# Filling the edge tile of x1 on VectorE behind the third block's candidates, instead of on GpSimd and VectorE ahead of step 1

## The chip, the cores and the metric

The kernel runs on one core of a Trainium2 chip. The core has five engines, each with its own instruction stream that it works through in order: TensorE (PE in the profile, with PEld for its weight loads), VectorE (DVE), ScalarE (ACT), GpSimd (POOL) and SyncE (SP). An instruction that needs another engine's result waits for that engine's semaphore, and everything behind it in its own stream waits with it. The metric is the device time of one execution in microseconds (us), smaller being better.

## The reference

A graph network with two layers works on 2708 nodes with 256 features. Cut to what matters here:

```python
# layer 0
x = _layernorm(x + relu(concatenate([x, adj @ x], axis=1) @ weight + bias))
# layer 1: two steps
R = S + eye(N);  R = R / R.sum(-1, keepdims=True)      # S is adj again
for n in range(2):
    q = Xa @ W1.T @ W2.T;  k = Xa @ W3.T
    probs = softmax(q @ k.T)
    # keep, in each row, the largest probabilities until their sum reaches 0.9
    A = probs * mask;  A = A / A.sum(-1)
    Xf = R @ Xf;  Xa = A @ Xa
    Z = Z + Xf @ U1[n].T + Xa @ U2[n].T
h = X + Z                                              # then two layer norms
```

The output of layer 0 is called x1 below. The product `A @ Xa` of the first step, with `Xa = x1`, is where the tile of this change is used.

## The kernel before, in words

**Tiling.** The 2708 nodes are cut into NB = 22 blocks of 128 rows. The last block, number EDGE = 21, has only 20 rows. `x1` is one tile of 128 partitions by 22 blocks by 256 features. A weight block `e` holds one row block of attention weights, 128 by 2708, padded to 2720 columns. For a product on TensorE it must be transposed in pieces of 128 columns. `columns(e, k)` cuts them out; the last piece starts at 2720 - 128 = 2592, so that the 20 last nodes lie in it at places 96 to 115 (AT = 96). The matching right-hand side can't be `x1[:, 21, :]`, in which these rows lie at partitions 0 to 19. So there is a second tile, `x1_edge`, 128 by 256, which is zero but for the 20 last rows of x1 at partitions 96 to 115. `part_y` (L566) takes it as the right-hand side of the last piece; the profile calls it `yg`, since it is cut out of the same room as the tile `yg`.

**The room.** `y_room` (L504) lies where layer 0's input `xT` lay. It holds the two buffers of `yg` for the sparse product, some spare columns, and `x1_edge`. The names of the second `Lists` use the second buffer of `yg` as well.

**Stages.** Layer 0 runs first, over the 22 blocks in a loop that ends at L499. While it runs, the columns of the adjacency matrix that hold anything are named, and two objects `Lists` (blocks 0 to 15, blocks 16 to 21) collect these names. `lists.end()` of the first one, right behind the loop, writes the names through memory: VectorE computes the target places `to` (L350), GpSimd sends seven scatters (L354), each of which waits until the one before it has landed, and then loads the finished list into `ix` (L357). Next come the lines of this change (L508, L509). Then step 1 begins, and after it step 2.

**The order around the change** is written out by hand: a manual schedule keeps, on each engine, the order in which the program names its instructions. The framework only adds the waits that the data need. The head of step 1 (L896 to L909) is this, where `begin1(t, 2)` writes three pairs of logits (TensorE L527, copied out by ScalarE L534) with six calls of `u1_project` in between (TensorE L670, ScalarE L673, and two stores by SyncE L674, L675):

```python
    begin1(0, 2)
    extract1(0)
    begin1(1, 2)
    part = exps1(0)
    part(0), part(1)
    begin1(2, 2)
    lists.take(0, 2)
    ra = finish1(0)
    extract1(1)
    part = exps1(1)
    part(0), part(1)
    for t in range(n_u, NB):
        u1_project(t)
    extract1(2)
```

`extract1(t)` is VectorE's: the eight largest of each of 16 segments of a row (L589, the "candidates"), their maximum (L613, L615) and 64 of them in order (L596, L598). `exps1(t)` is ScalarE's: the exponentials of these (L630) and of the whole row (L632), which need that maximum. `lists.take` is VectorE's (L330, L331), for the second list. `finish1(t)` is VectorE's: sums over the ordered values (L646 to L653), and the cut of the row at its threshold (L654). Its L651 reads column 0 of `sums`, the tile `xs`, which GpSimd clears once at L603, behind everything of `lists.end()`.

Behind this head the loop over the 22 blocks begins: in each pass TensorE transposes one block of weights (L554), ScalarE copies the pieces out (L556), and TensorE multiplies them by x1 (L583), while logits, exponentials and thresholds of the next blocks go on. GpSimd gathers the named rows of the adjacency matrix for the sparse product (L376, two blocks for each of the first two passes, one for each pass behind them), adds the identity (L378), and SyncE loads and stores its tiles (L373 to L390).

Of the kernel before, what the change touches and what calls it, by code (L numbers as in the profile page):

```python
# [41 lines left out]
AT = 96  # L42
# [19 lines left out]
def gnn_two_layer_kernel(ctx: ExitStack, tc: tile.TileContext, N, xT_d, x_d, adj_d, w0_d, b0_d,  # L62
# [72 lines left out]
    with fast:  # L135
        fast_path(fast, tc, c, flags, fint, xT_d, x_d, w0_d, b0_d, w1_d, w2_d, w3_d, u1_d, u2_d, g_d, b_d)
# [22 lines left out]
def fast_path(ctx, tc, c, flags, fint, xT_d, x_d, w0_d, b0_d, w1_d, w2_d, w3_d, u1_d, u2_d, g_d, b_d):  # L159
    nc = tc.nc  # L160
    N, D, DA, NB, DC, KH, CHS, rows = c.N, c.D, c.DA, c.NB, c.DC, c.KH, c.CHS, c.rows
# [66 lines left out]
    x1 = big.tile([P, NB, D], FP, tag="x1", name="x1")  # L228
# [11 lines left out]
    EDGE = NB - 1  # L240
# [264 lines left out]
    yg = y_room[:, :YW].rearrange("p (s c d) -> p s c d", s=2, d=D)  # L505
    spares = [y_room[:, YW + D * i:YW + D * (i + 1)] for i in range(4)]
    x1_edge = y_room[:, YW + 4 * D:YW + 5 * D]
    nc.gpsimd.memset(x1_edge, 0.0)  # L508
    nc.vector.tensor_copy(x1_edge[AT:AT + rows(EDGE)], x1[:rows(EDGE), EDGE, :])  # L509
    lists = Lists(ML, NB, flags[:, NF - 2:], yg[:, 1].rearrange("p c d -> p (c d)"))  # L510
    lists.turn()
    x1_transpose(NB - 1)
# [73 lines left out]
    def seg_max(dst, src, p, step, width):  # L586
        for i in range(NS):
            w = min(width, N - SEG * i) if step == SEG else width
            nc.vector.max(dst[:p, i * 8:(i + 1) * 8], src[:p, i * step:i * step + w])  # L589

    def put_in_order(dst, n, cand, p):

        spare = small.tile([P, NS2 * 8], FP, tag="spare", name="spare", bufs=1)[:, :cand.shape[1]]
        src = cand
        for i in range(0, n, 8):
            nc.vector.max(dst[:p, i:i + 8], src[:p])  # L596
            if i + 8 < n:
                nc.vector.match_replace(spare[:p], dst[:p, i:i + 8], src[:p], -3.0e38)  # L598
                src = spare
# [6 lines left out]
    def extract1(t):  # L606
        p = rows(t)
        e = es[t % 4]
        cand = small.tile([P, NS2 * 8], FP, tag="cand", name="cand", bufs=2)[:, :NS * 8]
        seg_max(cand, e, p, SEG, SEG)  # L610
        cv = cand.rearrange("p (s k) -> p s k", k=8)
        nmax = small.tile([P, 1], FP, tag="nmax", name="nmax", bufs=3)
        nc.vector.tensor_reduce(nmax[:p], cv[:p, :, 0], AX.X, ALU.max, negate=True)  # L613
        srt = small.tile([P, TOP1 + 1], FP, tag="srt", name="srt", bufs=3)
        nc.vector.tensor_reduce(srt[:p, TOP1:], cv[:p, :, 7], AX.X, ALU.max)  # L615
        put_in_order(srt, TOP1, cand, p)
        st1[t] = (nmax, srt)
# [48 lines left out]
    def u1_project(t):  # L666
        p = rows(t)
        pz = ps_acc()
        for j in range(DC):
            nc.tensor.matmul(pz[:p], lhsT=x1T[:, j, t * P:t * P + p],  # L670
                             rhs=c.u1[:, j].rearrange("p s e -> p (s e)"), start=j == 0, stop=j == DC - 1)
        o = v_out[:p, t % VS]
        nc.scalar.copy(o.rearrange("p s d -> p (s d)"), pz[:p])  # L673
        nc.sync.dma_start(out=c.yf_d[:p, t, :], in_=o[:, 1, :])  # L674
        nc.sync.dma_start(out=c.v_d[:p, t, :], in_=o[:, 0, :])  # L675
# [231 lines left out]
    for t in range(n_u, NB):  # L907
        u1_project(t)
    extract1(2)  # L909
    ends = None  # L910

    at = {(m // 2, 3 * (m % 2) + 1): m for m in range(4)}
# [844 lines left out]
```

## Time and profile before

| what | value |
|---|---|
| median of 3 runs | 1281.5 us (1278.85 to 1284.95) |
| the profiled execution's own time | 1286.8 us |
| its span (first to last instruction) | 1284.9 us |
| mean granted TensorE clock | 0.975 of full speed |
| PE busy | 1202.1 us, 94% |
| DVE busy | 973.9 us, 76% |
| ACT busy | 735.1 us, 57% |
| POOL busy | 634.9 us, 49% |

Step 1's head lies between about 280 and 348 us of the span, and the 22 passes follow. In the stretch from 312 to 325 us PE is busy for 0.36 us. Rows of the timeline give the start, the duration, the engine, the line and operation, the output and the input tile, how many instructions are merged, and in brackets how long the engine sat idle before it and who released it. Rows of the waits give who waited for whom: us in total, how often, and the longest. L12 is line 12 of the kernel file.

### The profile page before, as it was taken

The page shows a single profiled execution, that of the slowest core. Times are in us where ns is not written, and L with a number is a line of the kernel's source. Part 1 is how long each engine was busy: PE and PEld are TensorE (multiplying, and loading weights), DVE is VectorE, ACT ScalarE, POOL GpSimd, SP SyncE. Part 2 cuts the span into 40 slices and gives each one's busy share as a digit, 9 for nine tenths or more (in the row PEclk, how much of TensorE's full clock was granted, in tenths as well). Part 3 has the DMA queues.
Part 4 walks back from the last instruction along what each step waited for, and adds up shares of the span by engine and source line. Part 5 has one row for each costly group of instructions (what it writes and reads, how often), then busy time and mean ns, then how long its engine had stood idle before and what let it go on. Part 6 is the DMA issues. An engine that isn't in the chain of part 4 may idle for free.

```text
span 1284.9 us, 18709 instructions
## 1 busy us (share of the span) xinstructions
PE 1202.1 (94%) x5772; PEld 904.3 (70%) x5772; DVE 973.9 (76%) x3253; ACT 735.1 (57%) x1299; POOL 634.9 (49%) x597
## 2 busy tenths in 40 slices
PE   8999999987799999999999978999998999999885
PEld 6888888842377777777777646777766777776664
DVE  2455554973999998988871278979878999999886
ACT  2000111032566666666665498887888999989821
POOL 1000000004076552577766068878774878888860
PEclk9999999989899999999999888999999999999997
DMA  7455544523322220133334154665664555555451
GB/s 197 149 197 172 160 151 153 172 82 98 100 80 92 61 68 32 41 94 94 91 89 107 50 152 152 181 187 178 183 150 122 173 160 163 169 185 160 144 135 39
DMA packets 101703, 165.99 MB, mean 129 GB/s; under 512 B 17362, under 2 KB 74070, under 8 KB 101594
## 3 DMA queue, kind: packets, MB, share of 16 engines
q1 hardware_dynamic: 75308, 108.65, 26.1%
q0 software_dynamic: 20544, 51.17, 14.8%
q10 hardware_dynamic: 5742, 4.89, 1.3%
q8 instruction: 48, 0.79, 0.3%
q14 instruction: 61, 0.50, 0.1%
HBM read 130.74 MB, written 33.90 MB: 128 GB/s over the span
## 4 chain that ended last, share of the span: by engine, by line
PE 71%; DVE 10%; ACT 7%; DMA 6%; issue 3%; POOL 2%; SPq 0%; POOLq 0%; ACTq 0%; DVEq 0%
PE acc L583 23%; PE acc L266 16%; PE lg L527 8%; PE misc L769 6%; PE tr L554 6%; DMA yg<-yf_d,ix 3%; PE acc L670 2%; DMA yg<-v_d,ix 2%; DVE e L1110 2%; PE misc L402 2%; ACT e L988 2%; PE acc L691 2%; PE misc L441 2%; PE misc L719 2%; PE acc L477 1%
## 5 line engine op out<-in xcount | busy, mean ns | idle before, releaser
L556 ACT COPY wT<-tr 128x512 f32<-128x512 f32 (+2 forms) x258 | 136.6, 537 | 205.8 <-PE tr L554 205.8
L583 PE MATMUL acc<-ya,wT 128*128 128x256 f32 x924 | 223.1, 383 | 0.0
L739 POOL DMA_INDIRECT yg<-v_d,ix x154 | 193.5, 1256 | 59.3 <-issue 25.3
L583 PE MATMUL acc<-x,wT 128*128 128x256 f32 x882 | 217.4, 386 | 0.0
L739 POOL DMA_INDIRECT yg<-yf_d,ix x154 | 190.7, 1239 | 48.3 <-issue 26.2
L266 PE MATMUL acc<-y,adj_t 128*128 128x257 f32 x924 | 206.1, 382 | 0.0
L769 PE MATMUL misc<-yg,adj_t 128*128 128x256 f32 (+1 forms) x704 | 187.9, 398 | 18.1 <-DMA yg<-yf_d,ix 7.2
L583 PEld LDWEIGHTS acc<-x,wT 128*128 128x128 f32 x882 | 159.0, 190 | 58.1 <-issue 24.7
L583 PEld LDWEIGHTS acc<-ya,wT 128*128 128x128 f32 x924 | 172.1, 191 | 38.2 <-issue 16.7
L266 PEld LDWEIGHTS acc<-y,adj_t 128*128 128x128 f32 x924 | 174.9, 191 | 27.3 <-issue 1.9
L376 POOL DMA_INDIRECT adj_t<-in_adj,ix x154 | 168.4, 1094 | 50.9 <-issue 39.5
L769 PEld LDWEIGHTS misc<-yg,adj_t 128*128 128x128 f32 (+1 forms) x704 | 123.6, 191 | 69.6 <-issue 23.2
L527 PE MATMUL lg<-k,q 64*128 64x512 f32 (+3 forms) x528 | 138.0, 600 | 27.4 <-ACT e L534 13.5
L554 PE MATMUL tr<-ident,e 128*128 128x128 f32 (+1 forms) x946 | 145.2, 272 | 6.9 <-ACT wT L556 4.6
L554 PEld LDWEIGHTS tr<-ident,e 128*128 128x128 f32 (+1 forms) x946 | 117.7, 141 | 40.5 <-ACT wT L556 8.8
L343 POOL DMA_DIRECT2D part_d<-e x1 | 0.6, 573 | 278.6 <-DVE e L342 278.6
L988 ACT ACTIVATE e<-e,st 128x2708 f32<-128x2708 f32 (+1 forms) x43 | 113.5, 2640 | 0.1
L991 ACT ACTIVATE e<-e,st 128x2708 f32<-128x2708 f32 (+1 forms) x42 | 111.0, 2642 | 0.1
L454 ACT COPY x1T<-tr 128x256 f32<-128x256 f32 (+1 forms) x22 | 8.0, 365 | 179.8 <-PE tr L453 179.8
L589 DVE MAX8 cand<-e 128x8 f32<-128x170 f32 (+1 forms) x352 | 86.9, 318 | 15.9 <-ACT e L534 15.7
L1052 DVE MAX8 cand<-w 128x8 f32<-128x170 f32 (+1 forms) x352 | 94.1, 321 | 0.0
L527 PEld LDWEIGHTS lg<-k,q 64*128 64x128 f32 (+1 forms) x528 | 39.3, 183 | 59.1 <-issue 20.7
(246 smaller groups left out, 1749.6 us busy)
## 6 DMA issues: line engine op xcount, KB each, us to landing
adj_t<-in_adj SPq DMA_DIRECT2D x44, 704.0 KB
adj_t<-adjc_d SPq DMA_DIRECT2D x44, 448.0 KB
adjc_d<-adj_t SPq DMA_DIRECT2D x22, 256.0 KB
base<-za_d SPq DMA_DIRECT2D x40, 128.0 KB
adjc_d<-adj_t SPq DMA_DIRECT2D x22, 192.0 KB
xt<-in_x ACTq DMA_DIRECT2D x21, 128.0 KB
x_d<-x SPq DMA_DIRECT2D x21, 128.0 KB
x1b_d<-xb SPq DMA_DIRECT2D x21, 128.0 KB
```

The lines of the kernel that those rows point to most:

```text
L266: nc.tensor.matmul(acc[:p, :n], lhsT=halves[k // KH][:, k % KH, :p], rhs=y[:, k, :n], start=k == 0, stop=stop and k == NB - 1)
L376: nc.gpsimd.indirect_dma_start(out=a[:CW, i, :], out_offset=None, in_=adj_rows, in_offset=bass.IndirectOffsetOnAxis(ap=ix[:CW, m, i:i + 1] ...
L527: nc.tensor.matmul(lg[:p, h, at:at + b - a], lhsT=q[o, t * P:t * P + p], rhs=keys[s][o, i, :b - a], start=True, stop=True)
L554: nc.tensor.transpose(tr[:, k % 4, :p], columns(e[:p], k), ident[:p, :p])
L556: nc.scalar.copy(wT[:, :len(ks), :p], tr[:, :len(ks), :p])
L583: nc.tensor.matmul(acc[:p, :D], lhsT=wT[:, k % 4, :p], rhs=part_y(y, k), start=k == 0, stop=k == NB - 1)
L589: nc.vector.max(dst[:p, i * 8:(i + 1) * 8], src[:p, i * step:i * step + w])
L739: nc.gpsimd.indirect_dma_start(out=y[:CW, i, :], out_offset=None, in_=rows_d, in_offset=bass.IndirectOffsetOnAxis(ap=ix[:CW, m, i:i + 1], ...
L769: nc.tensor.matmul(acc[:p, :D], lhsT=a[:kw, k, :p], rhs=y[:kw, k, :], start=k == 0, stop=k == CC)
L988: nc.scalar.activation(scr[:b.p, :N], e, AF.Relu, bias=b.nz, scale=b.l[k], accum_out=b.relu)
L991: nc.scalar.activation(scr[:b.p, :N], e, AF.Sign, bias=b.nz, scale=b.l[k], accum_out=b.sign)
L1052: nc.vector.max(b.cand[:p, 8 * i:8 * i + 8], low[:p, SEG2 * i:SEG2 * (i + 1)])
```

## The change

The two instructions that fill `x1_edge` move. Before, GpSimd clears the tile (L508) and VectorE copies the 20 rows (L509), right behind the first `lists.end()` and ahead of step 1. After, VectorE does both, behind `extract1(2)`, the third block's candidates, just ahead of the loop over the blocks (L908 and L909 of the changed file; lines between the two places lie two lines higher there).

```diff
@@ -505,8 +505,6 @@
     yg = y_room[:, :YW].rearrange("p (s c d) -> p s c d", s=2, d=D)
     spares = [y_room[:, YW + D * i:YW + D * (i + 1)] for i in range(4)]
     x1_edge = y_room[:, YW + 4 * D:YW + 5 * D]
-    nc.gpsimd.memset(x1_edge, 0.0)
-    nc.vector.tensor_copy(x1_edge[AT:AT + rows(EDGE)], x1[:rows(EDGE), EDGE, :])
     lists = Lists(ML, NB, flags[:, NF - 2:], yg[:, 1].rearrange("p c d -> p (c d)"))
     lists.turn()
     x1_transpose(NB - 1)
@@ -907,6 +905,8 @@
     for t in range(n_u, NB):
         u1_project(t)
     extract1(2)
+    nc.vector.memset(x1_edge, 0.0)
+    nc.vector.tensor_copy(x1_edge[AT:AT + rows(EDGE)], x1[:rows(EDGE), EDGE, :])
     ends = None
 
     at = {(m // 2, 3 * (m % 2) + 1): m for m in range(4)}
```

## The prediction

> **What bounds the kernel now.** I read the page first. The fourth part, the chain that ended last, says that TensorE sets most of the time:
>
> ```profile
> PE 71%; DVE 10%; ACT 7%; DMA 6%; issue 3%; POOL 2%; SPq 0%; POOLq 0%; ACTq 0%; DVEq 0%
> ```
>
> So a change is worth what it does to stretches in which PE stands still, and the edit touches one. The waits between 285 and 400 us:
>
> ```profile
> DVE yg L509 <- POOL xs L603: 19.6, 1, 19.6
> ...
> PE lg L527 <- ACT e L534: 13.5, 2, 13.0
> ```
>
> These two are ends of one stall handed from engine to engine. The timelines of GpSimd, VectorE, ScalarE and TensorE show it:
>
> ```profile
> 292.02 0.93 POOL L354 DMA_INDIRECT list_d<-e,to  x1 [2.96 <-DVE to L350]
> ...
> 307.38 0.84 POOL L354 DMA_INDIRECT list_d<-e,to  x1 [1.39 <-DMA list_d<-e,to]
> 309.63 1.24 POOL L357 DMA_DIRECT2D ix<-list_d  x1 [1.41 <-DMA list_d<-e,to]
> 310.86 0.32 POOL L508 MEMSET yg<- 128x256 f32 x1
> 311.11 0.11 POOL L603 MEMSET xs<- 128x1 f32 x1
> ```
> ```profile
> 291.42 0.21 DVE L350 SCALAR_TENSOR_TENSOR to<-run,before_m,e 16x7 int32<-16x7 f32 x1
> 311.22 0.56 DVE L509 COPY yg<-x 20x256 f32<-20x256 f32 x1 [19.58 <-POOL xs L603]
> 311.79 3.88 DVE L589 MAX8 cand<-e 128x8 f32<-128x170 f32 x16
> ...
> 325.50 0.28 DVE L651 SCALAR_TENSOR_TENSOR qs<-xs,sc,srt 128x64 f32<-128x64 f32 x1
> ```
> ```profile
> 307.75 0.59 ACT L673 COPY v_out<-acc 128x512 f32<-128x512 f32 x1 [1.17 <-PE acc L670]
> 321.22 0.35 ACT L630 ACTIVATE srt<-srt,nmax 128x65 f32<-128x65 f32 x1 [12.88 <-DVE srt L596]
> ```
> ```profile
> 308.66 3.70 PE L670 MATMUL acc<-u,x1T 128*128 128x512 f32 x8
> 325.33 2.08 PE L527 MATMUL lg<-k,q 64*128 64x512 f32 x4 [12.96 <-ACT e L534]
> 327.34 4.56 PE L670 MATMUL acc<-u,x1T 128*128 128x512 f32 x8
> ...
> 342.11 5.46 PE L670 MATMUL acc<-u,x1T 128*128 128x512 f32 x8 [2.40 <-ACT v_out L673]
> ```
>
> GpSimd clears the tile at 310.86 only because the clear stands behind seven scatters that wait for one another. VectorE's copy waits for the clear, and behind the copy stands all of `extract1(0)`. ScalarE has nothing left but `exps1(0)`, which needs `extract1(0)`. TensorE has run until 312.36 and can't write the next logits, because ScalarE, stuck in front of `exps1(0)`, has not copied the last ones out. The chain of waits in order of time agrees: it runs through the clear, L509, L589, the sorting, L632, L654, the next L589 and the exponentials until 342.11, and from there on is nearly all PE.
>
> **The change part by part.** *The wait that goes.* VectorE is free at 291.63 (291.42 + 0.21). `extract1(0)` also needs its logits; ScalarE's last copy of them ran from 290.32 for 0.71, to 291.03. So it starts at about 291.6 instead of 311.79, and takes the same 9.3 us (311.79 to 321.10): done at 301.0. `lists.take` follows (321.10 to 323.5 before, 2.4 us) and ends at 303.4. So VectorE gains 20 us, but not all of it counts.
>
> *Who is late next.* ScalarE's order holds the six copies of `begin1(1, 2)` ahead of `exps1(0)`; the last of them ends at 308.34 (307.75 + 0.59), paced by TensorE. `exps1(0)` can't start before, and no longer has to wait: 308.34 instead of 321.22. **The gain is 321.22 - 308.34 = 12.9 us**; of VectorE's 20 us the other 7 become an idle wait for ScalarE. From there each row moves up by 12.9: the exponentials end at 311.5, `finish1(0)` starts at 311.5 (its first row stands at 324.41, 0.90 us idle behind ScalarE's L632), `extract1(1)` ends at 325.4 (338.31 before), `exps1(1)` starts at 325.5 (338.43), and the last two projections of TensorE, which wait for the copies behind `exps1(1)`, at 342.11 - 12.9 = 329.2.
>
> *TensorE in this stretch.* It loses the 13 us hole: the next logits start at 312.5, right behind 312.36. They and the following six projections then run warm: 1.13 for 2.08 and 3.70 for 4.56 us, 1.8 us less. That gives nothing, since 329.2 is set by ScalarE: the hole of 2.40 us before the last projections only grows, to 2.4 + 1.8 = 4.2 us or a little less. Sum of the holes, 15.4 before and about 4.2 after, and 1.8 of cold clock: 11.2 + 1.8 = 13.0, the same gain counted from the other side.
>
> *The clock behind the longer hole.* The row at 342.11 shows eight matmuls in 5.46 us where 3.70 is usual, so already the 2.40 us hole costs 1.76; the granted clock is 0.79 from 340 to 348 us. [...] I take 0. [...]
>
> *The two instructions in their new place.* The clear on VectorE: no row clears SBUF there, but L182 clears 128x257 in PSUM in 0.27 us; GpSimd's own clear took 0.32. The copy stays at 0.56. Together 0.83 us behind `extract1(2)`, whose end is 347.61 - 12.9 = 334.7; so `finish1(1)`, queued behind it, begins at 335.5 and ends at 340.2. What waits for it is the transposing of block 1, at 362.61 - 12.9 = 349.7, so 9.5 us of cover. `extract1(3)` waited 0.18 us for its logits, so 0.65 us of delay goes on; passes take PE 17.0 us, of which VectorE is busy 16.2, so it is gone after a pass or so. `x1_edge` itself is read first by L583 acc<-yg at 364.74 - 12.9 = 351.9, 16 us after the copy. Price: 0; without the cover 0.8.
>
> *GpSimd's side.* The removed clear frees 0.25 us. A wait remains that the clear used to hide: L651 of `finish1(0)` needs the cleared `xs`, which stands behind the same scatters. It is cleared at about 310.9 to 311.0. L651 falls 1.09 us behind the start of `finish1(0)`: 312.6. **So 1.6 us of cover**, and from there on each us by which the scatters get later costs one. Before, they ran beside an idle VectorE; now `extract1(0)` and `lists.take` run beside them. The nearest row for that is the first gather of the adjacency rows (313.91 to 322.4), which ran beside the same L589, L596, L598 and L330: all seven took 0.94 to 1.01 us, 0.30 apart. So I take no stretch. The other end is the second list, whose seven scatters ran beside a whole pass: from its L350 to the end of L357 it took 504.51 to 528.36, 23.9 us, against 291.63 to 310.87, 19.2 us. If all of that 4.6 us came here, 3.0 us of the gain would go.
>
> What stretched the second list is visible in the gathers:
>
> ```profile
> 381.97 3.04 DVE L654 SCALAR_TENSOR_TENSOR e<-e,th 128x2708 f32<-128x2708 f32 x1
> ```
> ```profile
> 382.12 3.71 POOL L376 DMA_INDIRECT adj_t<-in_adj,ix  x1 [0.30 <-issue]
> ```
>
> The gather under L654 takes 3.71 us instead of 0.95. [...] The row says 2.8 us, and decides. L654 of `finish1(0)` will run from 312.9 to 316.0, behind the last scatter, but over the first gather (from about 313.7). [...]
>
> *SyncE's queue and the rest.* The stores L674, L675 stand in the same order and follow ScalarE's copies; so do the loads L373 behind them, and all that the passes issue. Nothing in the passes is tied to the time at which the scatters end: the gathers' tile is waited for 13 us later than it comes.
>
> **Sum.** 12.9 + 0 + 0 + 0 = 12.9 us. On the profiled execution: span 1284.9 - 12.9 = 1272.0, own time 1286.8 - 12.9 = 1273.9. That execution lies 5.3 us above the median of the runs shown; taken off the median, 1281.5 - 12.9 = **1268.6 us**, 1.0% faster. A measurement of this kernel can tell about 0.5% (6.4 us) from no change, its three runs being spread by 0.24% to each side.
>
> **The rivals.** *The scatters stretch, and `xs` takes the place of the clear (B).* For it: L651's wait stands on the same queue, with only 1.6 us of cover, and the second list was 4.6 us slower beside VectorE. Against: no L654 falls into this stretch. Time: 4.6 - 1.6 = 3.0 us back, 1271.6 us.
>
> *They stretch so much that it ends slower (C).* Should the 8-largest searches block each scatter as L654 blocks a gather, 2.8 us each, the chain grows by 7 x 2.8 = 19.6 us, `xs` comes at 330.6, and L651 runs at 330.6 instead of 325.5: 5.1 us slower, 1286.6. It decides from 12.9 + 1.6 = 14.5 us of stretch on (2.1 us a scatter). Against it stand the seven unstretched gathers beside the same instructions.
>
> *The head start is lost later (D).* PE would arrive early at something that keeps its own time: the gathers, the stores, or the reading of the rows in the sparse product. For it: VectorE is busy 16.2 of 17.0 us in a pass and GpSimd 11 to 13, so little room is left to catch up. Against: the chain from 348 to 721 us is nearly all PE (367 of 373 us busy), and what it waits for is issued behind its own steps. All lost: 1281.5; half lost, 1275.
>
> **How the numbers follow.** My forecast has 0.80: its own range is 12.9 + 0.5 (clock) and + 2.5 (spread of the runs) to one side, which makes 1265.6, and 1.9 (clock) and 2 (spread) to the other, 1272.5. B 0.07, D 0.09 (half of it losing enough to come within 0.5%), C 0.04. The low end goes to 1265 and the high end to 1274, which takes in B with 2.4 us of spread and leaves D and C out. Faster by over 0.5%: 0.80 + 0.07 + 0.04 = 0.91; within: 0.05; slower: 0.04.
>
> **What would show it.** No idle row before VectorE's L589 at about 291.7, and one of about 8 us before `finish1(0)`, released by ScalarE; `exps1(0)` at about 308.3; no hole in PE at 312; one of about 4 us near 325; PE's first transposes of the passes at about 334.6 (347.50 before); the clear and copy behind the third candidates in under 1 us; then the passes 12.9 us earlier row by row. Wrong if L651 waits for GpSimd (B, C: scatters longer than 0.85 + 1.4 us apart), if the matmuls behind the 4 us hole take over 5.5 us, or if waits of PE in the passes grow (D).

## The result

The changed kernel takes 1272.47 us (median of 5 runs, 1269.54 to 1272.67), against 1281.5 us before (median of 5, 1278.85 to 1284.95). The ratio is 0.9922, with a 95% interval of 0.9901 to 0.9943: by the ratio 10.0 us faster, 7.3 to 12.7; the two medians differ by 9.0. The forecast was 12.9 us faster, 1268.6 us, within 1265 to 1274. So the direction and the mechanism hold, and the size is some 3 to 4 us too large; the experiments below show which term was mis-sized.

The profiled execution has a span of 1270.7 us and a time of 1272.57 us. The chain that ended last, by engine:

```profile
PE 73%; DVE 11%; ACT 7%; DMA 5%; POOL 2%; issue 2%; ACTq 0%; POOLq 0%; DVEq 0%
```

The timelines of the changed kernel answer to those of before. GpSimd:

```profile
289.84 0.93 POOL L354 DMA_INDIRECT list_d<-e,to  x1 [3.07 <-DVE to L350]
...
307.44 1.24 POOL L357 DMA_DIRECT2D ix<-list_d  x1 [1.65 <-DMA list_d<-e,to]
308.67 0.11 POOL L601 MEMSET xs<- 128x1 f32 x1
...
314.91 2.58 POOL L376 DMA_INDIRECT adj_t<-in_adj,ix  x1 [0.30 <-issue]
```

The scatters still wait for one another, but no clear of the edge tile stands behind them. The gather at 314.91 is the one that ran longer, beside L652 (L654 before). VectorE, where the row of the candidates leaves out the first two of the sixteen:

```profile
289.86 3.37 DVE L587 MAX8 cand<-e 128x8 f32<-128x170 f32 x14
...
312.26 0.21 DVE L644 TENSOR_SCALAR sc<-z 128x1 f32<-128x1 f32 x1 [11.17 <-ACT e L630]
...
313.35 0.28 DVE L649 SCALAR_TENSOR_TENSOR qs<-xs,sc,srt 128x64 f32<-128x64 f32 x1
...
335.55 0.27 DVE L908 MEMSET yg<- 128x256 f32 x1
335.86 0.29 DVE L909 COPY yg<-x 20x256 f32<-20x256 f32 x1
```

The first candidates now run beside the scatters, and the wait sits in front of the first finish, released by ScalarE. ScalarE and TensorE:

```profile
308.58 0.59 ACT L671 COPY v_out<-acc 128x512 f32<-128x512 f32 x1 [1.18 <-PE acc L668]
309.07 0.35 ACT L628 ACTIVATE srt<-srt,nmax 128x65 f32<-128x65 f32 x1
```
```profile
309.49 3.70 PE L668 MATMUL acc<-u,x1T 128*128 128x512 f32 x8
313.18 1.13 PE L525 MATMUL lg<-k,q 64*128 64x512 f32 x4
...
318.62 7.13 PE L668 MATMUL acc<-u,x1T 128*128 128x512 f32 x16
329.96 5.46 PE L668 MATMUL acc<-u,x1T 128*128 128x512 f32 x8 [4.20 <-ACT v_out L671]
```

The exponentials follow the last copy without a wait, the 13 us hole is gone, and the hole ahead of the last two projections has grown from 2.40 to 4.20 us.

### The profile page after: what moved, and what is told of

It reads as the page before. It is cut to its first block, busy times and chain, and to the rows that moved or that the text cites. A ratio compares the mean times of both kernels' runs of the same rounds, so it can differ in the third digit from the quotient of the medians.

```text
span 1270.7 us, 18706 instructions
## 1 busy us (share of the span) xinstructions
PE 1197.5 (94%) x5772; PEld 902.7 (71%) x5772; DVE 974.2 (77%) x3254; ACT 735.0 (58%) x1299; POOL 636.9 (50%) x596
## 4 chain that ended last, share of the span: by engine, by line
PE 73%; DVE 11%; ACT 7%; DMA 5%; POOL 2%; issue 2%; ACTq 0%; POOLq 0%; DVEq 0%
PE acc L581 25%; PE acc L266 16%; PE lg L525 8%; PE misc L767 7%; PE tr L552 6%; DMA yg<-yf_d,ix 3%; PE acc L668 2%; DVE e L1110 2%; PE misc L402 2%; PE acc L689 2%; DVE w L1105 2%; ACT e L988 2%; PE misc L441 2%; PE misc L717 2%; DMA yg<-v_d,ix 2%
## 5 line engine op out<-in xcount | busy, mean ns | idle before, releaser
L737 POOL DMA_INDIRECT yg<-yf_d,ix x154 | 190.1, 1234 | 48.3 <-issue 23.1
L767 PE MATMUL misc<-yg,adj_t 128*128 128x256 f32 (+1 forms) x704 | 184.9, 394 | 18.1 <-DMA yg<-yf_d,ix 8.1
L1105 DVE MATCH_REPLACE8 w<-part,e 128x680 f32<-128x680 f32 (+1 forms) x88 | 74.3, 850 | 0.0
```

What stands on the lines that cost most here:

```text
L737: nc.gpsimd.indirect_dma_start(out=y[:CW, i, :], out_offset=None, in_=rows_d, in_offset=bass.IndirectOffsetOnAxis(ap=ix[:CW, m, i:i + 1], ...
L767: nc.tensor.matmul(acc[:p, :D], lhsT=a[:kw, k, :p], rhs=y[:kw, k, :], start=k == 0, stop=k == CC)
L1105: nc.vector.match_replace(w[:b.p, W * i:W * (i + 1)], b.part[:b.p, i, :], e2(b.t)[:b.p, W * i:W * (i + 1)], 3.0e38)
```

## The experiments

**1. Which part of the change does it.** The theory: VectorE's stream was held by its copy, which waited for a clear at the end of GpSimd's queue, so that anything that breaks this link gives the whole gain. The rivals: it is the clear on GpSimd itself, or the place of the copy. One run times the change again, one leaves the clear where it was and moves the copy alone, one leaves both in place and changes the engine of the clear alone.

The copy alone moved:

```diff
     x1_edge = y_room[:, YW + 4 * D:YW + 5 * D]
     nc.gpsimd.memset(x1_edge, 0.0)
-    nc.vector.tensor_copy(x1_edge[AT:AT + rows(EDGE)], x1[:rows(EDGE), EDGE, :])
...
     extract1(2)
+    nc.vector.tensor_copy(x1_edge[AT:AT + rows(EDGE)], x1[:rows(EDGE), EDGE, :])
```

The engine of the clear alone changed:

```diff
-    nc.gpsimd.memset(x1_edge, 0.0)
+    nc.vector.memset(x1_edge, 0.0)
     nc.vector.tensor_copy(x1_edge[AT:AT + rows(EDGE)], x1[:rows(EDGE), EDGE, :])
```

The change again, with no edit:

> The changed kernel once more, timed closely beside the kernel before. If the wait behind the scatters is the whole story, 12.9 us less than before (ratio 0.990), with the head of step 1 (TensorE from the last projections ahead of the hole to the first transposes of the passes) shorter by 13 us. If something later gives part of it back, the head is shorter by 13 us, but the time by 8 us or less, and the passes or the stages behind them are longer than before by the difference.

The copy alone:

> Only the copy moves: GpSimd goes on clearing the tile behind its scatters, VectorE copies behind the third candidates. Theory (VectorE's stream was held by the copy, wherever the clear stands): the same gain as the change, 12.9 us within 0.5, since the clear is only waited for 20 us later, and xs is cleared 0.25 us later, inside its cover. Rival (the clear on GpSimd is what costs): near the time before, 1281.

The engine alone:

> Only the engine of the clear changes: VectorE clears and copies in the old place ahead of step 1. Theory: the wait for GpSimd's queue goes all the same; VectorE starts the first candidates 0.6 to 0.8 us later than with the change, inside its 8 to 11 us of idle time before the first finish, so the same gain, 12.9 us within 0.5. Rival (the place matters, since the copy reads x1's last rows or stands ahead of the candidates): less than half of the gain.

Measured, all on the same chip, with a median of 1280.02 us before (28 runs): the change 1270.71 (ratio 0.9929, 0.9908 to 0.9950); the copy alone 1271.66 (0.9936, 0.9913 to 0.9959); the engine alone 1271.38 (0.9933, 0.9910 to 0.9955). The three are one within their intervals: by the ratios 8.2 to 9.1 us faster than before. Neither the place nor the engine matters by itself; the link does. In the run with both early, VectorE's two instructions cost 0.6 us ahead of the candidates, and the cover swallows it:

```profile
289.07 0.27 DVE L508 MEMSET yg<- 128x256 f32 x1
289.38 0.28 DVE L509 COPY yg<-x 20x256 f32<-20x256 f32 x1
289.68 3.88 DVE L589 MAX8 cand<-e 128x8 f32<-128x170 f32 x16
...
311.10 0.21 DVE L646 TENSOR_SCALAR sc<-z 128x1 f32<-128x1 f32 x1 [9.69 <-ACT e L632]
```

But the gain is 8 to 9 us in each, where 12.9 within 0.5 was expected, and neither alternative of the first expectation explains that yet.

**2. Is GpSimd's queue still a limit? (rival B)** In the changed kernel, forty clears of the edge tile hold back the clear of `xs`:

```diff
+    for _ in range(40):
+        nc.gpsimd.memset(x1_edge, 0.0)
     nc.gpsimd.memset(sums[:, 0:1], 0.0)
```

> The changed kernel with forty clears of the edge tile on GpSimd (0.25 to 0.32 us each, 10 to 13 us together) between the scatters and the clear of xs. If L649 of the first finish waits on GpSimd's queue as the prediction's rival B says, xs comes 10 to 13 us later, of which the cover in the changed trace (308.8 to 313.35) takes 4.6: 5.4 to 8.2 us slower than the change, with VectorE idle ahead of L649. If GpSimd's queue is no longer on the path, no slower than the change.

Measured: 1282.38 us, ratio 1.0017 (1.0005 to 1.0029), 11.3 us slower than the change by the two ratios, where 5.4 to 8.2 was expected. The clears took 14.7 us, more than the 10 to 13 expected, being 0.37 us apart. GpSimd's and VectorE's timelines:

```profile
308.50 14.70 POOL L602 MEMSET yg<- 128x256 f32 x40
323.13 0.10 POOL L603 MEMSET xs<- 128x1 f32 x1
```
```profile
323.27 0.28 DVE L651 SCALAR_TENSOR_TENSOR qs<-xs,sc,srt 128x64 f32<-128x64 f32 x1 [10.02 <-POOL xs L603]
```

Of the 14.7 us, cover took 4.7 (from 308.67 to 313.35 in the changed kernel), and VectorE stood still for the other 10.0. TensorE's first transposes of the passes start 10.4 us later than with the change (345.76 for 335.35). So rival B's link is real, and what lies past its cover came through nearly in full (10.0 us of stall, 10.4 us later); in the changed kernel it simply does not bind. It had 4.7 us of cover, where the prediction gave it 1.6.

**3. Where are the missing 3 to 4 us?** The first profile of before took 1286.8 us, 6.8 us above the median of the 28 later runs. The same kernel was profiled twice more, without an edit:

> The kernel before, profiled once more, since the profiled execution that the prediction rests on lies 6.8 us above the median of 28 later runs of it. If the stall is the same in each execution, the hole in TensorE ahead of step 1's second logits is 13.0 us again and the head of step 1 lasts 67 us; the excess of the first profile then lies elsewhere. If the first profile had an unusually long chain of scatters, the hole is 1 to 4 us shorter, and so is the gain that can be had: 9 to 12 us.

> The same again, a third look at the kernel before, to see how much the chain of scatters and the hole vary from one execution to the next: by under 0.5 us if the waits are fixed, by 1 to 4 us if the scatters' landing times set them.

These two single executions took 1283.31 and 1277.50 us. In TensorE's timeline the hole is shorter in both, the first row being of the second profile, the other of the third:

```profile
324.00 2.08 PE L527 MATMUL lg<-k,q 64*128 64x512 f32 x4 [10.21 <-ACT e L534]
```
```profile
322.61 2.08 PE L527 MATMUL lg<-k,q 64*128 64x512 f32 x4 [8.82 <-ACT e L534]
```

The hole is a difference of two times, and both can be read in each of the three profiles of before (us):

| | first profile | second profile | third profile |
|---|---|---|---|
| first scatter starts | 292.02 | 290.54 | 289.51 |
| edge tile's clear starts | 310.86 | 309.53 | 308.14 |
| TensorE goes on (L527) | 325.33 | 324.00 | 322.61 |
| TensorE had been done since | 312.36 | 313.79 | 313.80 |
| hole | 12.96 | 10.21 | 8.82 |

From the first scatter to the clear it is 18.6 to 19.0 us, and from the clear until TensorE goes on 14.47 us in all three. So the chain of scatters was not unusually long in the first profile, as one of the expectations had it. What moves is the rest: TensorE was done 20.3 us behind the first scatter in the first profile, and 23.3 and 24.3 in the others. Most of the cause is in the same timelines, of the first profile:

```profile
268.90 5.33 PE L263 MATMUL acc<-y,adj_t 128*20 128x257 f32 x44 [3.42 <-issue]
...
280.07 1.13 PE L527 MATMUL lg<-k,q 64*128 64x512 f32 x4
281.13 3.70 PE L670 MATMUL acc<-u,x1T 128*128 128x512 f32 x8
```

of the second profile:

```profile
268.33 2.78 PE L263 MATMUL acc<-y,adj_t 128*20 128x257 f32 x44 [3.42 <-issue]
...
279.73 2.08 PE L527 MATMUL lg<-k,q 64*128 64x512 f32 x4
281.74 4.51 PE L670 MATMUL acc<-u,x1T 128*128 128x512 f32 x8
```

and of the third, in which the slow stretch is split between the two places:

```profile
267.70 4.16 PE L263 MATMUL acc<-y,adj_t 128*20 128x257 f32 x44 [3.42 <-issue]
...
281.01 5.26 PE L670 MATMUL acc<-u,x1T 128*128 128x512 f32 x8
```

In all three TensorE runs for a while at a lower clock, behind the hole of 3.42 us at the end of layer 0 or some microseconds later, behind gaps of about 2 us (2.00 and 1.87 us in the second profile, 1.88 in the third). In the first profile that stretch fell on layer 0's last block (5.33 for 2.78 us; 0.50 granted from 268 to 274 us), and the head of step 1 began at full clock (1.00 granted from 280 to 286 us). In the other two at least part of it fell on TensorE's last steps ahead of the logits (L441 took 1.36 and 1.35 us for 0.77) and on the head (0.72 and 0.65 granted from 280 to 286 us), so that TensorE was done later while the scatters were not held back. Twelve profiles of this case fit: where the matmuls of layer 0's last block took 5.33 or 5.34 us, the first eight projections took 3.70 (three profiles); where they took 2.78 to 4.47, the projections took 4.51 to 5.26 (six), but for the three with the idle matmuls of experiment 4, which have 3.70. Not all of it is the clock, though. The difference to the first profile's hole, in terms taken from the timelines (us):

| term | second profile | third profile |
|---|---|---|
| first logits start later behind VectorE's last norm (L155) | 0.7 | 0.6 |
| TensorE's work in the head takes longer | 1.8 | 2.5 |
| counts come back from memory sooner (VectorE's wait at L348: 5.86 in the first profile, then 5.40 and 5.00) | 0.5 | 0.9 |
| first scatter to clear takes less | -0.2 | 0.2 |
| hole shorter by | 2.8 | 4.1 |

The first two rows are the steps of TensorE that the slow stretch fell on, the other two are the time of transfers through memory. What placed the slow stretch no run here shows.

The changed kernel has no such hole, so for it the head's length is TensorE's and VectorE's work alone. Seven profiles, cut at the first logits and the first transposes of the passes (us):

| kernel | head of step 1 | passes and all behind |
|---|---|---|
| before, first profile | 67.4 | 937.4 |
| before, second profile | 66.4 | 935.2 |
| before, third profile | 64.1 | 932.5 |
| change | 56.3 | 935.4 |
| change again | 56.1 | 935.2 |
| copy alone | 54.4 | 930.3 |
| engine alone | 56.7 | 938.4 |

The head is 10.1 us shorter on the mean of four against the mean of three (55.9 and 66.0), and the stages behind it are the same on the mean (934.8 and 935.0). So no loss behind the head is seen (rival D), though one of a microsecond or two would be lost in the spread of single executions, 930.3 to 938.4. There was less to win: the 12.96 us hole is the longest of those seen. Between the two profiles whose heads both began at full clock (1.00 granted from 280 to 286 us), the first of before and the copy alone, the head is 13.0 us shorter, as long as that hole.

**4. Forcing the clock.** Four idle matmuls, whose results nothing reads, keep TensorE busy where it waits for VectorE in layer 0's last steps:

```diff
+    warm = ps_misc()
+
+    def keep_warm():
+        for _ in range(2):
+            nc.tensor.matmul(warm, lhsT=ident, rhs=x1T[:, 0, :CH], start=True, stop=True)
+
+    keep_warm()
     lists.turn()
+    keep_warm()
     x1_transpose(NB - 1)
```

in the kernel before, and in the changed one:

> The kernel before with four idle matmuls of 128x512 (about 0.9 us each, results unread) where TensorE waits for VectorE in layer 0's last steps, so that it comes into the head of step 1 at full clock more often. Theory: the end of the hole is set by the first scatter (33.1 to 33.5 us behind it in three profiles of the kernel before), not by TensorE; a quicker head only makes the hole longer, 12 to 13 us instead of 8.8 and 10.2, and the time stays that of the kernel before, within 1 us (or is up to 1 us longer, where the idle matmuls hold up the transposes). Rival (TensorE's clock in the head is worth its 2 us in any case): 2 us faster.

> The changed kernel with the same four idle matmuls. Theory: the head has no hole any more that could swallow a quicker TensorE, so it is faster than the changed kernel by the cold clock it avoids, 1 to 2.5 us, near 1269, and the difference to the run before it is 11 to 13 us, where it is 9 without the idle matmuls. Rival (the clock in the head has nothing to do with the gain's size): the same 9 us between the two.

These ran on a chip on which the kernel before takes 1320.11 us (23 runs), the added time lying behind the head, so only ratios and heads are compared. Before with idle matmuls: 1319.05 us, ratio 0.9998 (0.9974 to 1.0022). Changed with idle matmuls: 1307.50 us, 0.9915 (0.9879 to 0.9950). The heads came in at full clock, as meant (1.13 and 3.70 us for their first rows, as at 1.00 granted in the first profile). That before is no faster for it, as the theory has it, is what the ratio says, but its interval of about 3 us to each side does not rule out the rival's 2 us. The hole of before with idle matmuls is not the expected 12 to 13 us:

```profile
322.53 2.08 PE L535 MATMUL lg<-k,q 64*128 64x512 f32 x4 [10.64 <-ACT e L542]
```

The scatters took only 17.6 us to the clear in that execution (290.50 to 308.05), and the arithmetic of the table gives just this, 308.05 + 14.48 - 311.88 = 10.65. Of the 2.3 us that it is shorter than the first profile's, 1.3 are this quicker chain; 1.0 comes from first logits that start 3.0 us behind L155 instead of 2.0, with the idle matmuls ahead of them. The passes begin at 344.70 and 334.11 us, 10.6 apart, which is the hole, and the changed kernel's head lasts 54.5 us, 1.8 less than the 56.3 of the changed kernel whose head began at a lower clock (0.76 granted from 280 to 286 us). So the hole is what the change wins, but the clock alone does not fix its size; the landing times of the scatters do too. By the intervals, the timing can't tell the 11 us between these two from 9, so that question stays open.

**5. The next wait.** With the change, VectorE waits 11 us for ScalarE, which takes the first block's exponentials only behind six copies, and TensorE later waits 4.2 us for the second block's. ScalarE can take them in parts, between the copies; the clear of `xs` goes to the program's start, so that the earlier finish does not meet it:

```diff
-    def begin1(t, n):
+    def begin1(t, n, part=None):
...
-            for _ in range(n):
+            for j in range(n):
                 u1_project(n_u)
                 n_u += 1
+                if part and i and j == 0:
+                    part(i - 1)
...
-    begin1(1, 2)
-    part = exps1(0)
-    part(0), part(1)
+    begin1(1, 2, exps1(0))
```

> The changed kernel, in which ScalarE no longer takes the first block's exponentials behind all six copies of the second block's head, but in two parts between them (behind the fourth projection's first copy and the sixth's), and GpSimd clears xs at the start of the program. VectorE's 11 us wait ahead of the first finish should shrink to about 7, and the second block's candidates end 4 us earlier, at 322, when ScalarE still has copies until 323: its second exponentials start at 323 instead of 326.3, TensorE's hole of 4.2 us shrinks to about 1, and the matmuls behind it run warm (3.7 for 5.5 us): 4.5 to 5 us faster than the change. If the hole were due to something else, no gain; if ScalarE's parts hold up TensorE's copies, 1 to 2 us less of it.

Measured: 1267.04 us, ratio to before 0.9904 (0.9888 to 0.9921). That is 3.2 us faster than the change by the two ratios, where 4.5 to 5 was expected; their intervals overlap (the change has 0.9908 to 0.9950), so by time alone this gain is not certain. VectorE's wait shrank to 4.69 us, and in TensorE's timeline both the hole and the slow matmuls behind it are nearly gone:

```profile
308.21 0.21 DVE L644 TENSOR_SCALAR sc<-z 128x1 f32<-128x1 f32 x1 [4.69 <-ACT e L630]
```

```profile
325.92 3.81 PE L668 MATMUL acc<-u,x1T 128*128 128x512 f32 x8 [0.81 <-ACT v_out L671]
```

The head lasts 49.4 us and began at full clock (1.13 and 3.70 us for its first rows), 5.1 less than the 54.4 of the copy alone, which began at full clock too: the expected gain, in one execution of each.

Then the second block's exponentials are split as well:

```diff
     part = exps1(1)
-    part(0), part(1)
-    for t in range(n_u, NB):
+    part(0)
+    u1_project(n_u)
+    part(1)
+    for t in range(n_u + 1, NB):
         u1_project(t)
```

> As the run before it, and the second block's exponentials are split around the first of the remaining projections' copies as well, so that TensorE gets its accumulators back in time: no hole at all ahead of the last two projections, 1 us faster than the run before, 5.5 to 6 us faster than the change. If ScalarE is the limit there, the same time as that run.

Measured: 1262.57 us, ratio 0.9875 (0.9853 to 0.9898): by the ratio 16.0 us faster than before (the median of before is 1280.35 beside these runs, 17.8 above), and the fastest version found. By the two ratios it is 6.9 us faster than the change, and the two intervals do not overlap; those of this run and of the run before it do (3.7 us apart, where 1 was expected). TensorE has no hole in the head:

```profile
318.02 0.83 PE L527 MATMUL lg<-k,q 64*128 64x330 f32 x4
318.78 10.68 PE L668 MATMUL acc<-u,x1T 128*128 128x512 f32 x24
329.39 0.66 PE L554 MATMUL tr<-ident,e 128*128 128x128 f32 x4
```

The same version with the four idle matmuls, on the slower chip:

> The version with both exponentials between the copies, with the same four idle matmuls: 1 to 2.5 us faster than without them, 1260 to 1261.5, if the head of step 1 is TensorE's alone there; the same time if not.

Measured: 1303.75 us, ratio 0.9860 (0.9831 to 0.9889). Against 0.9875 that is 1.9 us better, but the intervals overlap and the chips differ: inconclusive by time. In the two profiles the head lasts 48.3 us instead of 50.2.

## Why the prediction was right, and where its size was off

- *The chain of waits.* Right, link by link. VectorE starts its candidates right behind `to`; ScalarE's exponentials start at 309.07, on the heels of the copy (308.3 predicted); TensorE goes on at 313.18 (312.5 predicted) without a hole.
- *Only ScalarE's part of VectorE's gain counts.* Right: VectorE waits 11.17 us ahead of the first finish (8 predicted), since it had begun 2.2 us sooner and ScalarE ended 0.8 us later than reckoned.
- *The hole ahead of the last projections grows to 4.2 us, and the clock costs nothing more.* Right in both: 4.20 us, and the eight matmuls take 5.46 us as before, at the same granted clock (0.76 from 329 to 336 us, and from 341 to 348 us before). The 0.5 and 1.9 us that the range gives the clock to its two sides no run shows: behind holes of 4.20 to 4.25 us the eight matmuls took 5.46 us in four executions and 6.06 in one, which is 0 to 0.6 us more.
- *The two moved instructions.* 0.27 and 0.29 us, 0.6 us together instead of 0.83, and hidden. The copy takes half the 0.56 us that it took before, in its old place too (0.28 in the run with both early); why, no run shows.
- *GpSimd beside VectorE.* The scatters did not stretch: 18.8 us from the first to `xs`, as before to the clear. One gather took 2.58 us beside L652, where 0.95 is usual, so there is a stretch, as the prediction's row had it, but of 1.6 us instead of 2.8; the gather ahead of it ran its 0.95 us beside the same L652. Why the one was held up and the other not no run here shows. The sum's last 0 is right all the same: the gathers end at 322.5, and L378 waits for its load until 338.8 (until 350.9 before).
- *Rival B's cover.* 4.7 us instead of 1.6: it had been reckoned with the first profile's distance between the scatters and the finish, which moves as the hole does.
- *The term that failed* is the gain itself, 321.22 - 308.34 = 12.9 us. Both times came from one execution, and the prediction took them as fixed. They are the ends of two strands that run beside each other, GpSimd's scatters and TensorE's projections, and the slow stretch of TensorE's clock around the end of layer 0, and the time of transfers through memory, shift the one against the other. Two more executions have 10.21 and 8.82 us of hole, one with idle matmuls 10.64, and the mean head is 10.1 us shorter, where 12.9 was predicted. That the profiled execution was 5.3 us over the median was noted in the sum, but taken as a shift of everything; some 2 us of it lay in this head (67.4 us, against 65.3 on the mean of the other two).
- *The range.* 1272.47 us lies inside 1265 to 1274, but the upper side had been made wide for the clock behind the last hole and for scatters that stretch, neither of which came. That it also covered a hole shorter than the profiled one is luck.

## What to carry to other kernels

A cheap instruction that waits for another engine holds up all that is queued behind it: here a copy of 0.56 us, which waited 19.6 us, and behind it the candidates, at 311.79 us instead of 289.86. What that costs is only the part by which the engines next in the chain are not late for reasons of their own: VectorE's wait of 19.6 us was worth 8 to 10. All of it goes once the link is cut, by another engine or by another place; either will do (ratios 0.9929, 0.9936 and 0.9933). The size of such a stall is the difference of two strands. Where a profiled execution lies well off the median, profile the kernel again before that difference is taken for the gain. And when a stall goes, read at once who is waited for next: here ScalarE's order held another 7 us (6.9 by the two ratios).

## What was not expected of the hardware

- In a stretch without any change in the code, the same stall lasted 8.82, 10.21 and 12.96 us in three executions, as TensorE's slow stretch fell on one stage or the next and the transfers landed sooner or later.
- Holes of 2.28 to 2.40 us (three executions) and of 4.20 to 4.25 us (five) were followed by the same slow eight matmuls, 5.46 us for 3.70 (6.06 in one); one of 14.11 us, in the run with forty clears, by 5.96; holes of 0.81 and 1.32 us by 3.81.
- Forty clears of 128x256 in a row on GpSimd took 0.37 us each, where a single one shows 0.32.
